# Attention's planned time scaled by 0.9 and 1.1 for ten tiles, and the ends of the later tiles in eight half groups

## The chip, the cores and the metric

The kernel runs on one core of a Trainium2 chip. A core has five engines that work side by side, each through its own queue in order: TensorE (PE, matrix multiplication; its loads of weights are shown as PEld), VectorE (DVE), ScalarE (ACT), GpSimd (POOL) and SyncE (SP, which issues DMAs). Sixteen DMA engines move data. The metric is the device time of one execution in microseconds (us); the kernel before has a median of 1754.32 us over three runs, from 1749.43 to 1756.26.

## The reference

One layer of a graph network with 4096 nodes of 512 features, all in 32 bit floats. The adjacency matrix is sparse: about one entry in 256 is set, and the diagonal always is. Eight heads of 64 features attend from the target rows to the neighbours alone, then come a residual, a second normalisation, a feed-forward part with 2048 hidden units, another residual with x and a last normalisation.

```python
hs = layer_norm(h_source, ln1_scale, ln1_bias)
ht = layer_norm(h_target, ln1_scale, ln1_bias)
q = (ht @ Wq + bq).reshape(T, H, HD) / jnp.sqrt(jnp.float32(HD))
k = (hs @ Wk + bk).reshape(S, H, HD)
v = (hs @ Wv + bv).reshape(S, H, HD)
logits = jnp.einsum('thd,shd->hts', q, k)
logits = jnp.where(edge_mask[None] != 0, logits, NEG)
probs = jax.nn.softmax(logits, axis=-1)
ctx = jnp.einsum('hts,shd->thd', probs, v).reshape(T, D)
ht = ht + ctx @ Wo + bo
ht = layer_norm(ht, ln2_scale, ln2_bias)
ff = jax.nn.gelu(ht @ W1) @ W2
return ht + ff
...
x = _layernorm(x + layer(x, h_target, adj, ...), axis=-1)
```

## The kernel before

The kernel never forms the dense 4096 x 4096 logits. It makes a list of neighbours for each row, sorts the rows by the number of their neighbours, and treats them in 32 tiles of 128 rows. A tile has as many slots as its longest row has neighbours (its cap, from 11 to 39; 603 slots in all). For each slot, one indirect DMA, which POOL issues, gathers the key and the value row of that neighbour for all 128 rows of the tile.

The first stage, until about 290 us, projects x to keys and values, which go to a table in DRAM, while ACT and DVE read the adjacency of the first 16 x 128 rows (part A), and part of that of the rest (part B), and make their lists. The second stage, which the change touches, weaves four streams together: attention over the 32 tiles, the feed-forward part over 18 groups of tiles, the rest of part B's lists with their sort, and the loads of half of the feed-forward weights.

Tiles are numbered from 0 in the code. Tiles 0, 1, 2 and 31 are groups of their own; tiles 3 to 30 go in pairs, (3, 4), (5, 6), and so on. Their caps, from tile 0: 11, 13, 14, 15, 15, 16, 17, 17, 18, 19, 19, 20, 22, 23, 24, 39, 12, 38, 13, 24, 14, 23, 15, 22, 15, 20, 16, 19, 17, 18, 17, 18. Tiles 0 to 15 belong to part A, the others to part B. Part B's records are put in order by 16 scatters that POOL issues (L880), spaced by 4.5 units of planned time, and loaded again by SP (L1008).

**The order of the work.** A function `_weave` writes down the program's order. Each stream is a Python generator that emits some instructions and then yields the planned time that these are to stand for. The stream whose planned clock is lowest goes next. A stream that yields None sleeps until another has gone on, and its clock is then at least that one's. The planned times are only weights: a pair of tiles has 60 units (`UNIT`) of feed-forward and 60 units of attention, where `PACE` doesn't say otherwise. So `PACE` sets how much feed-forward stands between two steps of attention in PE's queue, and in the others.

**Attention** (`attention`) goes through a tile in groups of three slots, and yields twice in each group: each yield ends a half group. DVE multiplies the gathered keys with the queries (L1287) and adds them up (L1293), ACT takes the exponential (L1300), DVE scales two of the three values with it (L1234) and ACT the third (L1268), DVE adds values in pairs in some groups (L1238, L1241), and PE turns the scaled values and adds them up in PSUM (`cps`, L1247). Gathers are requested four groups ahead into a ring of 17 slots, 20 in part B. The planned time of a half group is `cost` times its slots; `cost` comes from L1276, and L1277 and L1278 scale it: 0.7 for tiles 1 to 4, 0.85 for tiles 5 to 8, 1 from tile 9 on.

**A tile's end** (`finish`) is a generator that goes one step at each half group of the tiles that follow. DVE sums and inverts the weights' sums (L1123 to L1130), ACT spreads them out (L1133), PE turns them (L1139), ACT copies the result (L1141), DVE multiplies `cps` with it (L1144), PE turns the target rows into PSUM and adds the output projection (L1153, L1157), ACT copies the sum (L1163), DVE takes the moments (L702, L685), POOL the power -1/2 (L692), DVE the shift (L697), ACT normalises (L1179), PE turns (L1188) and ACT writes `h2T` (L1192). Between the steps it waits for a number of half groups that depends on `slow`: 1 + slow before L1139, 1 + slow before L1144, 1 + 3 slow before L1153, one each before L1163, the moments, L692 and L697, and 1 + slow before L1188. In all that is 8 half groups with `slow` = 0 and 14 with `slow` = 1. `slow` (L1120) is 0 for tiles 0 to 6 and 1 for the others.

**Feed-forward** (`feed`) of a group can only begin when its `h2T` has been written; until then the stream sleeps, and a group from the fourth on that has slept adds 3 units. It has 16 steps for a pair: 8 of hidden units (PE L1407, then the gelu on ACT, L1410), and 8 of outputs (PE L1416), with PE's transposes for the residual (L1441) among them. Its end (`end`) normalises, and POOL scatters the rows to the output.

Of the kernel before, what the change touches and what calls it, by code (L numbers as in the profile page):

```python
# [443 lines left out]
def adj_resnorm_kernel(  # L444
# [88 lines left out]
    with tc.tile_pool(name="keep", bufs=1) as keep:  # L533
# [17 lines left out]
        with ExitStack() as late:  # L551
# [171 lines left out]
            def behind(ins):  # L723
                return tc.issue_after(ins[-1]) if ins else nullcontext()
# [349 lines left out]
            def step(gens, i):  # L1074

                if i in gens and next(gens[i], StopIteration) is StopIteration:
                    del gens[i]

            def request(k):


                while issued[0] <= min(k + AHEAD, len(SG) - 1):
                    issue(issued[0])
                    mine = set(range(place[issued[0]], place[issued[0]] + SG[issued[0]][2]))
                    for m in range(max(k - len(held_up), 0), issued[0]):
                        assert not mine & set(range(place[m], place[m] + SG[m][2]))
                    issued[0] += 1
# [28 lines left out]
            def finish(i, p, cps, group, hs, mv):  # L1116


                rec, tq, cap = recs[i], tqs.pop(i), TILES[i][1]
                slow = 0 if i < QUICK else 1  # L1120
                first = i == 0

                nc.vector.scalar_tensor_tensor(p[:, :cap, :], rec[:, E0:E0 + cap].unsqueeze(2)  # L1123
# [72 lines left out]
            def go_on():  # L1196
                for i in list(fronts):
                    step(fronts, i)
# [18 lines left out]
            def attention():  # L1217


                tails, pend, turns = [], [], []  # L1220

                def advance():
                    go_on()
                    for t in list(tails):
                        if next(t, StopIteration) is StopIteration:
                            tails.remove(t)

                def values(i, j0, n, kv, p, cps, after):

                    m = n - 1 if n == S else n
                    v4 = kv[:, :m, D:].rearrange("p j (h d) -> p j h d", h=H)
                    nc.vector.tensor_tensor(v4, v4, p[:, j0:j0 + m, :].unsqueeze(3)  # L1234
                                            .to_broadcast([P, m, H, HD]), ALU.mult)
                    slots = list(range(n))
                    if m > 1 and i >= ADDS and TILES[i][1] < (HEAVY if i > NA else 23):
                        nc.vector.tensor_add(kv[:, 0, D:], kv[:, 0, D:], kv[:, 1, D:])  # L1238
                        slots.remove(1)
                        if n == S and i >= DENSE and j0 // S % 2:  # L1240
                            nc.vector.tensor_add(kv[:, 0, D:], kv[:, 0, D:], kv[:, S - 1, D:])  # L1241
                            slots.remove(S - 1)

                    def turn():
                        for j in slots:
                            for c in range(KC):
                                nc.tensor.matmul(cps[:, c, :], kv[:, j, D + c * P:D + (c + 1) * P],  # L1247
                                                 ident, is_transpose=True,
                                                 start=j0 + j == 0 and c == 0,
                                                 stop=j0 + n == TILES[i][1] and j == slots[-1],  # L1250
                                                 skip_group_check=True)
                        if after is not None:
                            tails.append(after)

                    turns.append(turn)
                    held_up[:] = turns

                def add_up():
                    while turns:
                        turns.pop(0)()  # L1260
                    held_up.clear()

                def by_scalar(kv, lg):
                    pa = sp.tile([P, H], F32, name="pa")
                    nc.scalar.activation(pa, lg[:, S - 1, :], AF.Exp)
                    for hd in range(H):
                        v = kv[:, S - 1, D + hd * HD:D + (hd + 1) * HD]
                        newest[:] = [nc.scalar.mul(v, v, pa[:, hd:hd + 1]).ins]  # L1268

                request(0)  # L1270
                yield 0.0
                k = 0
                for group in GROUPS:
                    hs = []
                    mv = sp.tile([P, 2, 2], F32, name="mv2")
                    cost = 0.5 * UNIT * len(group) / 2 / sum(TILES[i][1] for i in group)  # L1276
                    if 0 < group[0] < 9:  # L1277
                        cost *= PACE[group[0] > 4]  # L1278
                    for i in group:
                        cps = ps.tile([P, KC, P], F32, name="cps", bufs=2)  # L1280
                        while k < len(SG) and SG[k][0] == i:
                            _, j0, n = SG[k]
                            while i not in tqs:
                                step(fronts, i)
                            kv, tq = kvs.pop(k), tqs[i]
                            with behind(closing[:1 if j0 < 2 * S else 2]):
                                nc.vector.tensor_tensor(kv[:, :n, :D], kv[:, :n, :D],  # L1287
                                                        tq[:, :D].unsqueeze(1)
                                                        .to_broadcast([P, n, D]), ALU.mult)
                            lg = sp.tile([P, S, H], F32, name="lg")  # L1290
                            latest[:] = [lg[:, 0, 0:1]]
                            with behind(closing if j0 == S else []):
                                logits[:] = [nc.vector.tensor_reduce(  # L1293
                                    lg[:, :n, :],
                                    kv[:, :n, :D].rearrange("p j (h d) -> p j h d", h=H),
                                    AX.X, ALU.add).ins]
                            if i != 1:
                                closing.clear()
                            if j0 > 0:
                                nc.scalar.activation(p[:, j0:j0 + n, :], lg[:, :n, :], AF.Exp)  # L1300
                            add_up()
                            if k > 0:
                                request(k - 1)
                            advance()
                            yield cost * n
                            if pend:
                                values(*pend.pop())
                                if i < QUICK:
                                    add_up()
                                if i < QUICK or i > NA:  # L1310
                                    request(k)
                            advance()
                            if j0 == 0:
                                p = sp.tile([P, MAXE, H], F32, name="p", bufs=1)
                                nc.scalar.activation(p[:, :n, :], lg[:, :n, :], AF.Exp)
                            if n == S:
                                by_scalar(kv, lg)
                            last = j0 + n == TILES[i][1]
                            after = finish(i, p, cps, group, hs, mv) if last else None
                            pend.append((i, j0, n, kv, p, cps, after))  # L1320
                            yield cost * n
                            k += 1
                values(*pend.pop())
                add_up()
                while tails:
                    advance()
                    yield 3.0
                verdict()
# [138 lines left out]
            DENSE = 21  # L1467
            QUICK = 7
            UNIT = 60.0
            PACE = (0.7, 0.85)  # L1470

            ed = all_edges()
            steps = 2 * NQ + 1
# [41 lines left out]
            def fill():  # L1515
# [4 lines left out]
                for cost in _take(ed, FILL * steps):  # L1520
                    yield cost

            att = attention()
            _weave((projections(), 0), (prepare(), 0), (fill(), 0))
            src.close()
# [58 lines left out]
```

## Time and profile before

| what | value |
|---|---|
| median of the runs | 1754.32 us |
| the profiled execution's own time | 1755.7 us |
| its span, from first to last instruction | 1754.0 us |
| last matmul's end | 1742.5 us |
| granted clock of PE, mean | 0.981 |
| PE idle in the whole span | 98 us |
| L1407 and L1416 on PE, hidden and output matmuls | 468.9 and 461.2 us |
| L1247 on PE, turning the values | 243.7 us |
| gathers of keys and values on POOL (L994) | 603, 800.6 us |
| last step of attention (L1247) | 1629 us |

The span is the time on the core between its first and last instruction; the profiled execution's own time has 1.7 us around it. Busy times of different engines run side by side and don't add up. PE's records are pipelined, so the start of one matmul to the start of the next tells its price better than its own length.

### The profile page before, as it was taken

The page shows a single profiled execution, that of the slowest core. Times are in us where ns is not written, and L with a number is a line of the kernel's source. Part 1 is how long each engine was busy: PE and PEld are TensorE (multiplying, and loading weights), DVE is VectorE, ACT ScalarE, POOL GpSimd, SP SyncE. Part 2 cuts the span into 40 slices and gives each one's busy share as a digit, 9 for nine tenths or more (in the row PEclk, how much of TensorE's full clock was granted, in tenths as well). Part 3 has the DMA queues.
Part 4 walks back from the last instruction along what each step waited for, and adds up shares of the span by engine and source line. Part 5 has one row for each costly group of instructions (what it writes and reads, how often), then busy time and mean ns, then how long its engine had stood idle before and what let it go on. Part 6 is the DMA issues. An engine that isn't in the chain of part 4 may idle for free. (4 is left out here: it accounts for less than half of the span.)

```text
span 1754.0 us, 22757 instructions
## 1 busy us (share of the span) xinstructions
PE 1655.5 (94%) x6994; PEld 1078.4 (61%) x6994; DVE 1421.2 (81%) x2450; ACT 1232.7 (70%) x3134; POOL 1034.1 (59%) x824
## 2 busy tenths in 40 slices
PE   7999896999899999998899999999999999999997
PEld 3444443776676766666566667666666666666665
DVE  6887796879898999996788989988989788999300
ACT  5776673679678888685667878777878677878311
POOL 1000155667666677888687787777787866784101
PEclk9999998899999999999999999999999999999999
DMA  9999988978888897778788888887877767775000
GB/s 353 360 391 358 363 275 307 336 265 291 281 293 307 298 341 251 245 231 260 235 305 288 294 267 289 298 272 228 270 247 255 253 223 258 223 259 191 24 1 27
DMA packets 141611, 461.02 MB, mean 263 GB/s; under 512 B 18036, under 2 KB 23048, under 8 KB 141480
## 3 DMA queue, kind: packets, MB, share of 16 engines
q0 software_dynamic: 96272, 342.33, 58.2%
q1 hardware_dynamic: 39504, 98.26, 15.8%
q10 hardware_dynamic: 5704, 18.89, 2.7%
q8 instruction: 58, 0.95, 0.2%
q14 instruction: 73, 0.60, 0.1%
HBM read 430.61 MB, written 28.79 MB: 262 GB/s over the span
## 5 line engine op out<-in xcount | busy, mean ns | idle before, releaser
L994 POOL DMA_INDIRECT kv<-kvd,rec x603 | 800.6, 1328 | 288.7 <-issue 117.6
L1407 PE MATMUL pf<-h2T,w 128*128 128x256 f32 (+1 forms) x2304 | 468.9, 358 | 6.1 <-ACT h2T L1192 5.9
L1416 PE MATMUL po<-w,gt 128*128 128x512 f32 x1024 | 461.2, 593 | 5.6 <-ACT gt L1410 5.6
L1407 PEld LDWEIGHTS pf<-h2T,w 128*128 128x128 f32 x2304 | 394.9, 192 | 67.9 <-issue 17.7
L1287 DVE TENSOR_TENSOR kv<-kv,tq 128x1536 f32<-128x1536 f32 (+2 forms) x211 | 351.9, 1678 | 70.5 <-DMA kv<-kvd,rec 65.7
L1268 ACT ACTIVATE kv<-kv,pa 128x64 f32<-128x64 f32 x1520 | 390.9, 336 | 4.1
L1293 DVE TENSOR_REDUCE lg<-kv 128x24 f32<-128x1536 f32 (+2 forms) x211 | 350.9, 1669 | 0.3
L1416 PEld LDWEIGHTS po<-w,gt 128*128 128x128 f32 x1024 | 187.2, 190 | 201.4 <-issue 192.2
L1247 PEld LDWEIGHTS cps<-ident,kv 128*128 128x128 f32 x1844 | 218.4, 143 | 93.7 <-issue 44.4
L1234 DVE TENSOR_TENSOR kv<-kv,p 128x1024 f32<-128x1024 f32 (+1 forms) x211 | 251.6, 1196 | 19.3 <-ACT p L1300 19.2
L1247 PE MATMUL cps<-ident,kv 128*128 128x128 f32 x1844 | 243.7, 278 | 24.2 <-DVE kv L1234 17.6
L692 POOL TENSOR_TENSOR n_rs<-n_ve,mhalf 128x2 f32<-128x2 f32 (+2 forms) x53 | 57.6, 1086 | 338.4 <-DVE n_ve L685 157.7
L740 ACT ACTIVATE kv<-kv 128x1024 uint8<-128x1024 int32 x128 | 134.4, 1053 | 56.4 <-DMA kv<-in_adj_dram 22.9
L1410 ACT ACT_TABLE_LOAD x108 | 138.6, 1283 | 1.9
L1410 ACT ACTIVATE gt<-pf 128x512 f32<-128x512 f32 x128 | 76.4, 597 | 75.4 <-PE pf L1407 71.9
L1157 PE MATMUL t<-wo,rb 128*128 128x512 f32 x256 | 119.6, 611 | 5.3 <-DVE rb L1144 5.3
L956 PE MATMUL pq<-wk,h2T 128*128 128x512 f32 x256 | 121.2, 618 | 3.0 <-ACT tq L958 1.6
L956 PE MATMUL pq<-wv,h2T 128*128 128x512 f32 x256 | 115.5, 594 | 3.7 <-ACT kv L958 2.2
L1047 PE MATMUL t<-wq,tq 128*128 128x512 f32 x256 | 115.0, 593 | 2.9 <-ACT tq L1040 2.9
L749 DVE MAX8 cand<-kv 128x8 uint16<-128x171 uint16 (+1 forms) x384 | 108.4, 326 | 1.0
L1300 ACT ACTIVATE p<-lg 128x24 f32<-128x24 f32 (+2 forms) x179 | 38.9, 217 | 92.4 <-DVE lg L1293 89.5
L956 PEld LDWEIGHTS pq<-wv,h2T 128*128 128x128 f32 x256 | 48.3, 190 | 66.3 <-issue 56.9
(165 smaller groups left out, 1587.6 us busy)
## 6 DMA issues: line engine op xcount, KB each, us to landing
kv<-in_adj_dram SPq DMA_DIRECT2D x128, 512.0 KB, 6.8
kvd<-tq ACTq DMA_DIRECT2D x23, 512.0 KB, 7.2
kv<-kvd,rec POOLq DMA_INDIRECT x603, 5.9
kv<-in_L_gnn_h_target_dram SPq DMA_DIRECT2D x32, 256.0 KB, 6.8
w<-in_L_gnn_W_dram SPq DMA_DIRECT2D x8, 1024.0 KB, 9.7
kv<-in_x_dram SPq DMA_DIRECT2D x15, 512.0 KB, 8.2
kvd<-kv ACTq DMA_DIRECT2D x9, 512.0 KB, 7.7
rest_d<-gid SPq DMA_DIRECT2D x32, 96.0 KB, 5.1
```

The source lines that it names most:

```text
L740: nc.scalar.activation(sg, a, AF.Sign, accum_out=dpart[:, i, h:h + 1])
L956: nc.tensor.matmul(pkv, hT[:, kc, j * P:(j + 1) * P], w[:, kc, :], start=kc == 0, stop=kc == KC - 1)
L994: issues[:] = [nc.gpsimd.indirect_dma_start(out=dst, out_offset=None, in_=table[:, :], in_offset=bass.IndirectOffsetOnAxis(ap=idx, axis=0) ...
L1157: nc.tensor.matmul(pa, ct[:, c, :], wo[:, c, :], start=False, stop=c == KC - 1, skip_group_check=True)
L1234: nc.vector.tensor_tensor(v4, v4, p[:, j0:j0 + m, :].unsqueeze(3) .to_broadcast([P, m, H, HD]), ALU.mult)
L1247: nc.tensor.matmul(cps[:, c, :], kv[:, j, D + c * P:D + (c + 1) * P], ident, is_transpose=True, start=j0 + j == 0 and c == 0, stop=j0 + n ...
L1268: newest[:] = [nc.scalar.mul(v, v, pa[:, hd:hd + 1]).ins]
L1287: nc.vector.tensor_tensor(kv[:, :n, :D], kv[:, :n, :D], tq[:, :D].unsqueeze(1) .to_broadcast([P, n, D]), ALU.mult)
L1293: logits[:] = [nc.vector.tensor_reduce(lg[:, :n, :], kv[:, :n, :D].rearrange("p j (h d) -> p j h d", h=H), AX.X, ALU.add).ins]
L1407: nc.tensor.matmul(pf[:, k, :], w1[(f0 + k) // KC][:, kc, (f0 + k) % KC * P:((f0 + k) % KC + 1) * P], h2T[:, kc, :w], start=kc == 0, stop= ...
L1410: nc.scalar.activation(gt, pf, AF.Gelu_apprx_tanh)
L1416: nc.tensor.matmul(po[j], gt[:, k, j * P:(j + 1) * P], w2[(f0 + k) // KC][:, (f0 + k) % KC, :], start=False, stop=f0 + k == FC - 1, skip_g ...
```

## The change

Three edits of constants and conditions; no instruction is added or taken away.

```diff
-                slow = 0 if i < QUICK else 1
+                slow = 0 if i < QUICK or i > 10 else 1
...
-                    if 0 < group[0] < 9:
-                        cost *= PACE[group[0] > 4]
+                    if 0 < group[0] < 19:
+                        cost *= PACE[(group[0] > 4) + (group[0] > 8) + (group[0] > 10)]
...
-            PACE = (0.7, 0.85)
+            PACE = (0.7, 0.85, 0.9, 1.1)
```

`group[0]` is the first tile of a group. The pair (9, 10) gets a planned time of 54 units for its attention instead of 60, and the four pairs (11, 12) to (17, 18) get 66 each. Tiles up to 8 and from 19 on keep theirs. The ends of tiles 11 to 31 take 8 half groups instead of 14; those of tiles 7 to 10 keep 14, and those up to tile 6 keep 8.

## The prediction

> **What bounds the kernel now.** I read the first part of the page, then the busy time of all engines in stretches of 50 us, then the waits of PE between 600 and 1640 us, and last the timeline around the longest of them.
>
> ```profile
> span 1754.0 us, 22757 instructions
> PE 1655.5 (94%) x6994; PEld 1078.4 (61%) x6994; DVE 1421.2 (81%) x2450; ACT 1232.7 (70%) x3134; POOL 1034.1 (59%) x824
> ```
>
> PE is the bound: its work and its idle time add up to the span. The change takes no work away, so the only things it can move are PE's idle 98 us and the clock that PE gets. The stretches (columns: PE, PEld, DVE, ACT, POOL busy, PE's clock, DMA share, GB/s) show where idle time is left:
>
> ```profile
> 650.00:700.00 50.00, 47.25 (x215) 32.13 (x215) 49.90 (x92) 39.10 (x100) 35.08 (x23) 1.00 0.81 271
> 700.00:750.00 50.00, 48.60 (x204) 31.44 (x203) 48.40 (x60) 35.59 (x95) 41.79 (x29) 1.00 0.74 241
> 750.00:800.00 50.00, 45.75 (x205) 31.69 (x204) 38.38 (x48) 34.94 (x93) 40.35 (x34) 1.00 0.76 242
> 800.00:850.00 50.00, 45.30 (x210) 31.94 (x211) 41.73 (x39) 34.08 (x96) 37.48 (x31) 0.97 0.74 233
> 850.00:900.00 50.00, 40.69 (x187) 28.60 (x186) 36.16 (x38) 33.13 (x103) 36.47 (x31) 0.93 0.82 273
> ...
> 1600.00:1650.00 50.00, 50.00 (x212) 33.94 (x211) 34.76 (x76) 30.31 (x80) 4.96 (x5) 1.00 0.11 35
> 1650.00:1700.00 50.00, 50.00 (x186) 33.30 (x185) 3.23 (x12) 10.99 (x22) 5.26 (x6) 1.00 0.07 21
> ```
>
> In 650 to 750 DVE is full (lists and tiles 9 and 10, counted from 0). From 750 to 900 PE idles 18.3 us of 150 and DVE is not full. From 1650 on there is feed-forward alone and PE never waits. Some 55 us of PE's idle time fall before 600 us or behind the last matmul, where the change does nothing.
>
> ```profile
> PE t L1037 <- ACT tq L1033: 10.4, 3, 7.9
> PE cps L1247 <- DVE kv L1238: 6.2, 6, 2.2
> PE cps L1247 <- DVE kv L1234: 6.1, 2, 5.9
> PE pf L1407 <- ACT h2T L1192: 5.9, 5, 2.2
> PE t L1188 <- ACT h L1179: 5.4, 4, 3.0
> ```
>
> (total us, times, longest.) Nothing waits at L1157, the output projection at the tile's end. The timeline of PE gives the two long gaps, and the price of a feed-forward step:
>
> ```profile
> 774.92 3.62 PE L1407 MATMUL pf<-h2T,w 128*128 128x256 f32 x16
> 778.38 3.60 PE L1416 MATMUL po<-w,gt 128*128 128x512 f32 x8
> 781.81 1.04 PE L1247 MATMUL cps<-ident,kv 128*128 128x128 f32 x8
> ...
> 804.70 2.82 PE L1247 MATMUL cps<-ident,kv 128*128 128x128 f32 x12 [5.88 <-DVE kv L1234]
> ...
> 879.60 1.11 PE L1037 MATMUL t<-ident,tq 128*128 128x128 f32 x4 [7.88 <-ACT tq L1033]
> ```
>
> Behind both stands POOL: DVE waits 7.9 and 8.9 us for gathers just before, since POOL issues one gather per 1.25 us without a break and has 16 record scatters (L880, 730 to 853 us) among them.
>
> **The planned clocks.** A pair's feed-forward is 8 hidden steps of 778.38 - 774.92 = 3.46 us, 8 output steps of 3.43 and 1.04 of transposes: 56.2 us for 60 planned units, 0.94 us each. A pair of tiles has 60 units of attention too. Before, the pairs from tile 9 on end at 276, 336, 396, 456, 516; after, at 270, 336, 402, 468, 534 and 18 later from there. Feed-forward of group g becomes ready a tile end behind. Fourteen half groups of some 2.4 units are 34, eight are 19: for groups from tile 19 on the 18 later and the 15 sooner nearly cancel. Followed through the weave's rule, feed-forward of group g (from 4 on) starts at 60 g - 45.1 in both until it sleeps once, at group 15 before (starting at 862.7), at group 10 after (560.7); its last group starts at 982.7 before and 980.7 after. So feed-forward is neither starved nor moved; attention is moved against it, first 6 units forward, then 24 back. The stretch of feed-forward alone at the end loses 18 x 0.94 = 17 us, which the middle gets.
>
> **Term A, 0.9 on tiles 9 and 10.** PE gets 5.6 us less feed-forward there, while DVE is the bound. DVE idles 4.4 us in 600 to 750 (50 - 47.30 in the first row not shown, then 0.10 and 1.60). If attention moves up into that, PE loses 5.6 - 4.4 = 1.2 us; if DVE takes no more, 5.6. I take 1.2, as DVE's idle time is there in the row. The lists' work is put behind attention by as much and has slack until the scatters.
>
> **Term B, 1.1 on tiles 11 to 18.** Four pairs get 5.6 us more feed-forward each, 22.5 in all, from 752 to about 1080 us. PE's gaps there, from the timeline: 0.86, 2.20, 5.88, 1.22, 7.88 up to 880, then 1.63, 2.20, 3.02, 2.31, in all 27.2. While POOL and DVE set the pace, each us of matmuls put in takes a us of gap. Up to 880 the first pair and two thirds of the second add 9.5 against 18.0; behind it 12 against 9.2, of which I leave 1 for handovers. Gain 9.5 + 8.2 = 17.7. Bounds: nothing, where the gaps are fixed distances between two instructions that both move, and 22.5. In the planned span of the scatters (301 to 369) attention reaches tile 14 three units later, so they share POOL with some 45 slots' gathers instead of 50: 5 x 1.25 = 6 us that help the same gaps and aren't added.
>
> The clock: in 805 to 810 us its row has 0.75 and in 875 to 885 0.58 and 0.74; some 3.3 us of matmuls ran at half speed behind each long gap, 1.6 us lost each. With 8.5 us of gaps left I count one: -1.6 (0 to -3.2). The Trainium skill (TensorE: Matmul & The Clock Gate, Part 1: The HAM clock gate) says that the clock halves after an idle window of about 3.4 us. The trace bears it out roughly (3.02 us at 1047 is not followed by it, 3.10 at 323 is), and by the rule both losses would vanish only if both gaps fall below that.
>
> **Term C, eight half groups.** Nothing is added; ACT's copies L1133 and L1141, DVE's product L1144, PE's L1139, L1153 and L1157, then the norm (DVE, POOL's power L692 past some gathers, ACT L1179) and PE's L1188 come sooner. No DMA is among them. The transposes L1139 and the projection L1157 stand 2 half groups apart instead of 6. Six early tile ends already run so; one waited:
>
> ```profile
> 454.09 0.60 PE L1139 MATMUL t<-ident,rb 128*128 128x128 f32 x4
> ...
> 463.80 0.58 ACT L1141 COPY rb<-t 128x512 f32<-128x512 f32 x1
> ...
> 464.41 0.69 DVE L1144 TENSOR_TENSOR rb<-cps,rb 128x512 f32<-128x512 f32 x1
> ...
> 465.15 5.89 PE L1157 MATMUL t<-wo,rb 128*128 128x512 f32 x8 [5.28 <-DVE rb L1144]
> ```
>
> ACT had 9.7 us of other work ahead. While PE waits there, the next attention transposes and feed-forward are queued behind it, and with them POOL's free slots. For the 21 tile ends from 11 on I took from the timeline how long L1139 to the end of L1144 lasts now (1.4 to 8.7 us) and a third of the distance from L1139 to L1157 (4.1 to 8.8). The first is longer at tiles 12, 14, 15, 16, 21 and 23, by 1.7, 3.7, 1.5, 1.1, 0.9 and 1.8: 10.7 us. At L1188 one half group of 2.8 us goes; where ACT's L1179 ended less than that ahead (groups 7, 8, 9 and 15, by 1.3, 0, 0 and 1.9) 8.0 us are lost. Of the 18.7, 15.1 are in the stretch where B takes away the lateness; I scale these with its idle time, 9.5 of 27.2, to 5.3, and keep 3.6: +8.9. Bounds: 0, as five of the six early ends show, and by the sixth: 5.28 and 3.4 us of half clock work, over six ends 1.45 a tile, 30 us in 21.
>
> At no cost: some 2.4 more gelus stand among exponentials, two table loads of 1283 ns each, 6 us of ACT, hidden by its 11 to 16 idle us in every 50. The Trainium skill (ScalarE: Activation LUTs, Table sets: the hidden batching unit) speaks against it: calls of one set belong together, and a switch is put at 2.66 us with a drain, which would make it 13. The timeline shows gelu 20 ns behind a load's end, so no drain.
>
> **The sum.** 1.2 - 17.7 - 1.6 + 8.9 = -9.2 against the profiled execution's 1755.7: 1746.5. That one was 1.4 above the median shown, so against the median 1745.1; I say 1745.
>
> **Rivals.** *The tile ends take the place of the gaps (slower).* For it: ACT and DVE run in order, and the end at 465 us; against it: lists burdened ACT then (its stretch 460 to 465 has 4.94 of 5 busy), and later ACT is busy 34 of 50. At 1.45 us for each of the 21 ends, and half of B: 1.2 - 8.9 + 30 = +22, 1776 against the median; at two thirds of that price +12, 1766. It decides from (17.7 + 1.6 - 1.2) / 21 = 0.86 us a tile on. *The gaps stay (no change).* The gaps follow POOL's queue and the record loads, which move along with attention; at 863 us POOL itself waited 5.1 us for a record load behind the last scatter. Against it: POOL's load per matmul falls. Then 1.2 + 3.6 less a few us: 1750 to 1759. *Nothing of C comes and B is whole:* 1.2 - 22.5 - 3.2 = -24.5, 1730.
>
> **How the numbers follow.** Forecast with its own range of 1736 to 1747: 0.38; the whole gain 0.10; no change 0.27; slower 0.25. About 0.5% is what a measurement of this kernel can tell from nothing, 1745.5 to 1763.1; the forecast's upper edge lies within it by little. So faster 0.47, same 0.28, slower 0.25. The range 1729 to 1769 leaves out the worst of the slower case and little of the gain.
>
> **What would show it.** B right: no PE gap over 3.5 us at 780 to 900, no row under 0.95 in the clock there, idle time of PE from 750 to 1080 under 12 us. A right: 1 to 6 us more PE idle in 650 to 750. C right: waits at L1157 and L1188 together of 5 to 14 us; over 20 and the slower rival has it. The stretch with DVE nearly idle at the end should be some 95 us long instead of 112. The forecast is wrong if that stretch shrinks and PE's idle time doesn't: then gaps moved instead of closing.

## The result and the profile after

The changed kernel takes 1746.65 us (median of 22 runs, 1739.93 to 1756.12) against 1753.93 us of the kernel before in the same jobs: ratio 0.9962, 95% interval 0.9949 to 0.9974. By the ratio that is 6.7 us less (the medians differ by 7.3), where 9.2 were predicted.

The first part of the page, of the changed kernel:

```profile
span 1739.8 us, 22750 instructions
PE 1654.6 (95%) x6994; PEld 1075.0 (62%) x6994; DVE 1421.7 (82%) x2450; ACT 1236.4 (71%) x3136; POOL 994.5 (57%) x824
```

The work is the same, 1654.6 us of PE against 1655.5; what went is idle time. The profiled execution is one of the shortest, 5 us under the median: it was 3 us ahead at 560 us, while the order on PE first differs near 617 us, so some 11 of the 14 us between the two spans arise where the kernels differ. The medians say 7; the rest is the spread between executions. The stretches of 50 us (columns as before):

```profile
650.00:700.00 50.00, 46.90 (x206) 31.47 (x205) 49.90 (x88) 42.73 (x112) 30.25 (x27) 1.00 0.82 285
700.00:750.00 50.00, 47.73 (x202) 30.90 (x200) 50.00 (x67) 38.69 (x98) 36.34 (x26) 1.00 0.68 224
750.00:800.00 50.00, 49.11 (x223) 34.39 (x223) 39.77 (x48) 37.95 (x103) 40.10 (x34) 1.00 0.77 247
800.00:850.00 50.00, 42.48 (x182) 27.90 (x181) 39.62 (x37) 33.95 (x94) 33.88 (x30) 0.93 0.71 231
850.00:900.00 50.00, 50.00 (x241) 36.13 (x240) 35.62 (x38) 33.52 (x88) 40.16 (x32) 1.00 0.86 290
...
1600.00:1650.00 50.00, 48.65 (x210) 32.93 (x209) 40.68 (x85) 35.39 (x89) 11.60 (x11) 1.00 0.24 81
1650.00:1700.00 50.00, 50.00 (x172) 31.43 (x171) 2.03 (x7) 6.38 (x12) 0.58 (x1) 1.00 0.02 6
```

From 750 to 900 PE now idles 8.4 us instead of 18.3, and nothing at all in the last 50 of these. In 650 to 750 it idles 5.4 instead of 4.2. The stretch 800 to 850 got worse, with a clock of 0.93. Attention's last matmul (L1247) ends at 1642.5 us of 1728.6, so feed-forward stands alone for 86 us. Before it was 104: the table ahead of the prediction gives 1629 us for attention's last step, but the trace has its last L1247 at 1638.1.

Where the feed-forward went can be counted in the two traces, with the prediction's prices of a step (3.46, 3.43 and 1.04 us). Between the last L1247 of tile 10 and that of tile 18 PE does 245.3 us of it instead of 224.6. Of these 20.7 us, 3.5 come from tiles 9 and 10 and 17.2 from the end. PE's idle time between the same two points fell from 29.6 to 14.2 us.

The waits of PE between 600 and 1640 us (total, times, longest):

```profile
PE t L1157 <- DVE rb L1144: 8.9, 2, 6.0
PE pf L1407 <- ACT h2T L1192: 7.7, 6, 2.4
PE cps L1247 <- DVE kv L1238: 7.1, 9, 1.7
PE t L1188 <- ACT tq L1040: 2.0, 2, 1.5
PE po L1416 <- ACT gt L1410: 1.4, 1, 1.4
```

The long waits for gathered values and for the queries are gone, and L1157, where nothing waited, leads the list. The other engines say that the relief is real. These are a wait of DVE, before and after, and one of POOL, before and after, in the same stretch:

```profile
DVE kv L1287 <- DMA kv<-kvd,rec: 48.7, 17, 8.9
...
DVE kv L1287 <- DMA kv<-kvd,rec: 29.3, 14, 5.3
...
POOL kv L994 <- PE cps L1247: 44.5, 51, 3.4
...
POOL kv L994 <- PE cps L1247: 69.3, 58, 6.2
```

DVE waits 29.3 us for gathers instead of 48.7, and POOL waits 69.3 us for PE to free slots instead of 44.5: POOL is ahead of PE more of the time. The longest gap that is left, at tile 12's end, in the timeline:

```profile
794.94 0.60 PE L1139 MATMUL t<-ident,rb 128*128 128x128 f32 x4
...
799.89 0.58 ACT L1141 COPY rb<-t 128x512 f32<-128x512 f32 x1
...
805.96 0.69 DVE L1144 TENSOR_TENSOR rb<-cps,rb 128x512 f32<-128x512 f32 x1
...
806.70 4.63 PE L1157 MATMUL t<-wo,rb 128*128 128x512 f32 x5 [5.98 <-DVE rb L1144]
```

It is a gap of the kind that stood at 465 us before, where ACT alone was late and DVE followed at once. Here ACT comes to its copy 4.3 us after the transposes and DVE to its product 5.5 us after the copy, and PE, which has the projection two half groups on in its queue, waits for it.

### The profile page after: what moved, and what is told of

Its sections match the earlier page's. It is cut to its first block, busy times and chain, and to the rows that moved or that the text cites. A ratio compares the mean times of both kernels' runs of the same rounds, so it can differ in the third digit from the quotient of the medians.

```text
span 1739.8 us, 22750 instructions
## 1 busy us (share of the span) xinstructions
PE 1654.6 (95%) x6994; PEld 1075.0 (62%) x6994; DVE 1421.7 (82%) x2450; ACT 1236.4 (71%) x3136; POOL 994.5 (57%) x824
## 5 line engine op out<-in xcount | busy, mean ns | idle before, releaser
L994 POOL DMA_INDIRECT kv<-kvd,rec x603 | 775.9, 1287 | 320.9 <-issue 115.3
L1407 PE MATMUL pf<-h2T,w 128*128 128x256 f32 (+1 forms) x2304 | 471.3, 359 | 7.8 <-ACT h2T L1192 7.7
L1407 PEld LDWEIGHTS pf<-h2T,w 128*128 128x128 f32 x2304 | 394.1, 192 | 64.9 <-ACT h2T L1192 12.5
L1247 PEld LDWEIGHTS cps<-ident,kv 128*128 128x128 f32 x1844 | 216.2, 142 | 89.7 <-issue 51.3
L1247 PE MATMUL cps<-ident,kv 128*128 128x128 f32 x1844 | 242.1, 276 | 17.5 <-DVE kv L1234 10.4
L692 POOL TENSOR_TENSOR n_rs<-n_ve,mhalf 128x2 f32<-128x2 f32 (+2 forms) x53 | 48.5, 915 | 313.4 <-DVE n_ve L685 170.7
L1157 PE MATMUL t<-wo,rb 128*128 128x512 f32 x256 | 123.8, 629 | 12.5 <-DVE rb L1144 12.5
```

The lines of the kernel that those rows point to most:

```text
L994: issues[:] = [nc.gpsimd.indirect_dma_start(out=dst, out_offset=None, in_=table[:, :], in_offset=bass.IndirectOffsetOnAxis(ap=idx, axis=0) ...
L1157: nc.tensor.matmul(pa, ct[:, c, :], wo[:, c, :], start=False, stop=c == KC - 1, skip_group_check=True)
L1407: nc.tensor.matmul(pf[:, k, :], w1[(f0 + k) // KC][:, kc, (f0 + k) % KC * P:((f0 + k) % KC + 1) * P], h2T[:, kc, :w], start=kc == 0, stop= ...
```

## The experiments

Each edit is shown against the changed kernel. All ratios are to the kernel before, with their 95% intervals.

| run | tiles 9, 10 | tiles 11 to 18 | half groups of the ends | ratio |
|---|---|---|---|---|
| before | 1 | 1 | 14 | 1 |
| changed | 0.9 | 1.1 | 8 from tile 11 | 0.9962 (0.9949 to 0.9974) |
| e1 | 0.9 | 1.1 | 14 | 0.9982 (0.9968 to 0.9997) |
| e2 | 1 | 1 | 8 | 1.003 (1.0013 to 1.0048) |
| e3 | 0.9 | 1 | 8 | 1.0111 (1.0096 to 1.0126) |
| e4, e11 | 0.9 | 1.1 | 14 to tile 14, then 8 | 0.9942 (0.9924 to 0.996), 0.9941 (0.9924 to 0.9958) |
| e5 | 0.95 | 1.1 | 8 | 0.9983 (0.9966 to 1.0001) |
| e6 | 0.9 | 1 | 14 | 1.0073 (1.0048 to 1.0099) |
| e7 | 0.9 | 1.05 | 8 | 1.0029 (1.0012 to 1.0045) |
| e8 | 0.9 | 1.1, and 0.95 on 19, 20 | as e4 | 0.9974 (0.9959 to 0.9988) |
| e9 | 0.9 | 1 | 14, lists from 64 | 1.0077 (1.0065 to 1.0089) |
| e10 | 0.9 | 1.1 | 10 | 1.0021 (1.0006 to 1.0036) |
| e12 | 0.9 | 1.1 | as e4, lists from 67 | 1.0018 (1.0004 to 1.0033) |

The trace of each run gives PE's idle time between 560 us and its last matmul, from the starts and ends of its matmuls, and half of the busy time that fell into records of half clock:

| profiled run | idle us | lost to half clock | sum | last matmul ends |
|---|---|---|---|---|
| before | 43.9 | 2.9 | 46.8 | 1742.5 |
| changed | 30.4 | 5.9 | 36.3 | 1728.6 |
| e1 | 33.6 | 10.0 | 43.7 | 1737.3 |
| e2 | 41.3 | 8.3 | 49.6 | 1743.3 |
| e3 | 47.7 | 7.6 | 55.3 | 1749.7 |
| e4 | 34.5 | 4.9 | 39.4 | 1733.8 |
| e5 | 33.6 | 9.7 | 43.3 | 1736.9 |
| e6 | 47.7 | 13.1 | 60.8 | 1755.0 |
| e7 | 40.9 | 12.7 | 53.6 | 1744.0 |
| e8 | 30.4 | 8.1 | 38.5 | 1735.2 |
| e9 | 39.7 | 17.2 | 56.9 | 1749.9 |
| e10 | 38.1 | 7.3 | 45.4 | 1738.9 |
| e11 | 30.3 | 6.0 | 36.3 | 1728.5 |
| e12 | 39.0 | 9.4 | 48.4 | 1743.2 |

The last column less the sum is 1690 to 1697 us in every row. So what these executions differ by behind 560 us is PE's gaps and its half clock, to within that spread of 6 us, which is as large as the change's gain. That says where the time went, not why. And each row is a single execution: those of the changed kernel, e3 and e10 are 5, 9 and 5 us faster than their medians, so the ratios above decide what an edit is worth.

**e1, the planned times alone.**

```diff
-                slow = 0 if i < QUICK or i > 10 else 1
+                slow = 0 if i < QUICK else 1
```

> The change with the tiles' ends as before (fourteen half groups from tile 7 on): terms A and B without C. Theory 1, the prediction's sum of independent terms: 1.2 - 17.7 - 1.6 = -18 us, ratio to before 0.990. Theory 2, B needs C: without the sooner ends feed-forward of the groups behind tiles 15 to 18 isn't ready in time (followed through the weave it sleeps at groups 9, 10 and 15 and its last group starts at planned 1000.7 instead of 982.7), so nothing is moved from the end into the middle: ratio 0.998 to 1.010, and the stretch of feed-forward alone at the end stays near 110 us. Theory 3, the gain is C's: ratio 1.00.

Theory 1's 0.990 is far outside the interval; the time is at the lower edge of theory 2's. And feed-forward stands alone for 104.1 us, as in the kernel before. A stretch of it:

```profile
1600.00:1650.00 50.00, 50.00 (x206) 33.75 (x205) 30.96 (x76) 27.45 (x74) 4.07 (x4) 1.00 0.07 24
```

In 1600 to 1650 DVE works 31 us here and 41 in the changed kernel: attention is over sooner against feed-forward. Nothing was moved from the end into the middle, as theory 2 had followed through the weave, where the groups sleep until their late h2T. Tiles 11 to 18 still have 13.8 us of feed-forward more than before, but 3.5 of it come from tiles 9 and 10 and 10.4 from tiles 19 to 31. What is left of the gain is local.

**e2, the ends alone.**

```diff
-            PACE = (0.7, 0.85, 0.9, 1.1)
+            PACE = (0.7, 0.85, 1.0, 1.0)
```

> Only the ends of tiles 11 to 31 in eight half groups, attention's planned times as before: term C alone. Theory 1: a loss, 8.9 us where B relieves the middle and up to 18.7 where it doesn't, ratio 1.005 to 1.011, with waits at L1157 and L1188 of 10 to 20 us together. Theory 2: the same sign, as nothing is moved. Theory 3, the sooner ends themselves free PSUM and the buffer of L1133 and so bring the gain: ratio 0.994 to 0.997.

A loss, 5.3 us, so theory 3 falls; it is smaller than theory 1 had it. Its waits, over the same part of PE's time:

```profile
PE t L1157 <- DVE rb L1144: 8.4, 3, 6.0
PE cps L1247 <- DVE kv L1234: 6.9, 3, 5.8
```

The gap at 801 us is still there (5.78), and one of 6.01 at L1157 (916 us) has come. Against this, feed-forward alone shrank to 96 us, as the sleep before group 15 went. By the table PE even idles less than before, 41.3 us against 43.9; what its sum has more is half clock, 8.3 us against 2.9. The mean granted clock says the same over all executions: 0.980 in the twelve of e2, 0.982 in the 23 of the kernel before beside them, which is up to 4 us.

**e3, without 1.1.**

```diff
-            PACE = (0.7, 0.85, 0.9, 1.1)
+            PACE = (0.7, 0.85, 0.9, 1.0)
```

> The change without 1.1: tiles 9 and 10 at 0.9, tiles 11 to 18 at 1.0, ends in eight half groups (terms A and C). Theory 1 and 2: ratio 1.005 to 1.012, 1 to 6 us above the run with the ends alone. The stretch of feed-forward alone at the end would be the longest of all, near 118 us. Theory 3: ratio 0.994 to 0.997, the whole gain without 1.1.

The ratio (of four runs) is as theories 1 and 2 said, but by another share: it is 14 us over e2, where term A was to be 1 to 6. The end was not the longest (99.8 us). From e3 to the changed kernel, 1.1 is worth 26 us.

**e4 and e11, the first four long ends back.**

```diff
-                slow = 0 if i < QUICK or i > 10 else 1
+                slow = 0 if i < QUICK or i > 14 else 1
```

> The change with the ends of tiles 11 to 14 in fourteen half groups again, those of 15 to 31 in eight. In the changed kernel the two long waits of PE (5.98 at 807 us, 2.93 at 912 us) stand at L1157 of tiles 12 and 14. If they are the price of the short distance (term C), they go with the half clock behind them: 8.9 us of waits and up to 5 us of clock, ratio to before 0.988 to 0.992. If they are lateness that shows wherever PE meets DVE next, the time stays that of the changed kernel, 0.995 to 0.998.

> The version with the ends from tile 15 on once more, for a narrower interval than 0.9924 to 0.9960: the same, 0.993 to 0.996. Under 0.9949 it would be outside the interval of the changed kernel (0.9949 to 0.9974).

Twice 0.994, faster than the kernel before by 10 us, and between what the two theories gave for e4. The interval of e11 and that of the changed kernel overlap (0.9949 to 0.9958), so that it beats the change too is likely and not shown. The waits of e11:

```profile
PE pf L1407 <- ACT h2T L1192: 9.0, 6, 2.6
...
PE po L1416 <- ACT gt L1410: 6.1, 3, 3.4
PE cps L1247 <- DVE kv L1234: 3.6, 3, 3.1
```

L1157 is off the list, but 3.1 us come back at the attention matmul (797 us) and 3.4 at a gelu (937 us). Some of the lateness was the short ends' price, some only showed there.

**e5 and e6, more and less of 0.9.**

```diff
-            PACE = (0.7, 0.85, 0.9, 1.1)
+            PACE = (0.7, 0.85, 0.95, 1.1)
```

> The change with 0.95 instead of 0.9 on tiles 9 and 10. Theory 1 (0.9 costs 1 to 6 us of feed-forward cover where DVE is full, so half of it comes back): ratio to before 0.993 to 0.996. Theory 2 (0.9 is worth its price when 1.1 follows: it brings attention forward, so that tiles 11 to 14 start sooner against the scatters and the record loads): ratio 0.997 to 1.000.

Theory 1 falls by little, and theory 2's number holds: with 1.1 behind it, 0.9 is 3.7 us better than 0.95, though the intervals overlap. Theory 2's reason is not shown by that. e6 has 0.9 alone, with the ends as before:

```diff
-                slow = 0 if i < QUICK or i > 10 else 1
+                slow = 0 if i < QUICK else 1
...
-            PACE = (0.7, 0.85, 0.9, 1.1)
+            PACE = (0.7, 0.85, 0.9, 1.0)
```

> Only 0.9 on tiles 9 and 10; tiles 11 to 18 at 1.0 and the ends as before: term A alone. The run without 1.1 was 14 us above the one with the ends alone, where the prediction gave A 1 to 6 us. If A itself has that price, ratio 1.006 to 1.010; if the price comes from the ends being short while attention is ahead of feed-forward, ratio 1.000 to 1.003.

Term A by itself costs 12.8 us. Three stretches and two waits of e6 show where:

```profile
650.00:700.00 50.00, 46.91 (x210) 32.21 (x209) 49.90 (x85) 41.22 (x107) 30.70 (x28) 1.00 0.81 284
700.00:750.00 50.00, 47.54 (x200) 30.17 (x199) 50.00 (x71) 38.08 (x97) 37.58 (x28) 1.00 0.71 238
750.00:800.00 50.00, 43.39 (x190) 28.81 (x188) 38.54 (x44) 33.10 (x96) 40.64 (x33) 0.96 0.70 235
```

```profile
PE cps L1247 <- DVE kv L1234: 14.4, 2, 8.6
...
PE t L1188 <- ACT h L1179: 7.6, 4, 4.3
```

In 650 to 750 PE loses 1.4 us more than before, as predicted. The rest comes later, and most of it in this execution is the clock. The gap at 802 us has grown from 5.9 to 8.6 and one of 5.8 stands at 900, but that of 7.9 at 880 is gone: from 750 to 1100 us PE idles 26.4 us, no more than before (28.2). The records have 37 us of half clock behind 560 us instead of 10. So of the 14.0 us that PE's sum is longer than before, 10.2 are half clock and 3.8 idle time. This execution had a lower clock than most; the mean over the seven of e6 is 0.978, over the 30 of the kernel before beside them 0.981, which is some 5 us of the 12.8 at most.

**e7, half of 1.1.**

```diff
-            PACE = (0.7, 0.85, 0.9, 1.1)
+            PACE = (0.7, 0.85, 0.9, 1.05)
```

> The change with 1.05 instead of 1.1 on tiles 11 to 18: half of B. If each us of feed-forward put into the middle takes a us of gap (the prediction's rule), the time lies halfway between the run without 1.1 (1.011) and the changed kernel (0.996): 1.002 to 1.005. If the gain hangs on the long gaps that halve the clock, it comes at once or not at all: 0.995 to 0.998, or over 1.007.

About halfway between e3 and the changed kernel (their mean is 1.0037): half of the pace brings about half of the gain, which does not hang on one gap. That each us of matmuls takes a us of gap is not shown by it. From e3 to e7, and again from e7 to the changed kernel, tiles 11 to 18 get 10.4 us more feed-forward; in the traces PE's idle time there falls by 4.3 us at the first step and by 11.4 at the second.

**e8, a lead for attention.** Against e4:

```diff
+                    elif group[0] == 19:
+                        cost *= 0.95
```

> A version to beat both: ends of tiles 15 to 31 in eight half groups, tiles 9 and 10 at 0.9, 11 to 18 at 1.1, and the pair of tiles 19 and 20 at 0.95, which lets attention lead feed-forward by 3 more units from there. In the run with the ends from tile 15, PE waited 10.6 us in 8 times at L1407 for h2T, since feed-forward takes each h2T as soon as it is written. If the lead takes these away: ratio 0.988 to 0.992. If the lateness shows at another wait: 0.993 to 0.996.

It brought nothing, and 5 to 6 us of e4's gain went, so both theories' ranges were missed. The waits for h2T fell from 9.3 us in e4 to 2.1, but those for a gelu rose from 5.5 to 8.3. A wait at L1407 of 2 us each is no gap that can simply be taken out.

**e9, are the lists the cause of e6?** Against e6:

```diff
-            WAIT = 70.0
+            WAIT = 64.0
```

> As the run with 0.9 alone (1.0073), but part B's lists, their sort and scatters start at planned 64 instead of 70, so that from tile 11 on attention and lists stand as in the kernel before to each other, both 6 units ahead of feed-forward. Theory L (0.9 costs 13 us since attention outruns the lists, and their DVE work and scatters fall on tiles 11 and 12): ratio 0.998 to 1.002, tile 12's end near 790 us instead of 802, the 8.6 us gap at 802 under 5. Theory F (it costs as 6 units of feed-forward are missing in PE's queue from there on): ratio 1.005 to 1.010, the gaps stay.

The gap came down to 6.3 us, as theory L had it in part, but it ended at 806 us instead of 802, and tile 12's last L1247 at 796.3 instead of 790.1. The time is that of e6; theory F's number holds. It doesn't prove F: PE's order differs from that of e6 from about 411 us on, and tiles 9 and 10 have 3.4 us less feed-forward, so more than the lists moved. Nor does PE idle more than in the kernel before (39.7 us against 43.9); what the table has more is half clock, 17.2 us.

**e10, two half groups more before the projection.**

```diff
-                for _ in range(0 if first else 1 + 3 * slow):
+                for _ in range(0 if first else 3 if i > 10 else 1 + 3 * slow):
```

> The change with the ends of tiles 11 to 31 in ten half groups: two more between the product L1144 and the projection L1153, the rest as in the change. If the waits at L1157 (8.9 us in 2 and the half clock behind) are the price of the short ends, they go and the ratio is 0.990 to 0.994. If what counts is when h2T is ready (feed-forward sleeps when it is late, 2 half groups are some 5 units), the waits go and the time doesn't: 0.997 to 1.002, with a stretch of feed-forward alone at the end of over 90 us.

The waits at L1157 fell from 8.9 to 0.9 us and the time got 10 us worse, just above what the second theory gave; feed-forward alone lasted 92 us.

```profile
PE t L1188 <- ACT h L1179: 8.3, 4, 7.2
```

PE now waits 7.2 us at once for the normalised rows (at 835 us), further on in the same end.

**e12, the lists sooner.** Against e4, `WAIT` at 67.

> The version with the ends from tile 15 on and the lists 3 planned units sooner. By theory L the lists' load on tiles 11 and 12 goes down a little and with it the remaining gap of 2.5 us at 799: ratio 0.990 to 0.994. If DVE, full from 600 to 750 us, only gets the lists' work sooner: 0.995 to 0.999.

Neither: 1.0018, 13 us over e4. Its trace has a gap of 9.1 us at 873 and one of 4.8 at 742, both of attention's matmul behind DVE. Three units in the lists' place cost as much here as 0.9 did in e6, while the six of e9 changed nothing against e6. Why, no run shows.

## Why the prediction was right, and where its steps were wrong

The forecast held in direction and size (-9.2 predicted, -6.7 measured), and the mechanism that it named first is shown: feed-forward put into tiles 11 to 18 (20.7 us, 22.5 predicted) closes PE's gaps there, and most of it comes out of the end, whose stretch is 18 us shorter (17 predicted). The terms, however, didn't hold singly.

- **Term B (-17.7 and -1.6 of clock).** Measured -16 us with long ends (e6 to e1) and -26 us with short ones (e3 to the change). Both stand beside 0.9, so they include what 1.1 takes back of A's price. The rule of a us of gap for each us of matmuls was too high in the traces: in the change 20.7 us more feed-forward took 15.4 us of idle time in tiles 11 to 18. From 750 to 1080 us idle time fell from 28.2 to 11.6, where I had asked for under 12.
- **Term A (1.2, at most 5.6) is the step that failed.** It measured 12.8 us alone and 14 with the short ends. I priced it in its own stretch, where it was right (1.2 to 1.4 us), and took it that the price ends there. But by the planned clocks attention then stays 6 units ahead of feed-forward through the tightest stretch, until something gives them back, and part of the price there is the clock: in e6's trace 10.2 us more of half clock, with no more idle time from 750 to 1100 us. In the change 1.1 gives the 6 units back, and then 0.9 costs nothing that shows (e5). Whether it is the missing matmuls or the work of the lists that falls on tiles 11 and 12 stays open; e9's number is that of the first, and it moved too much to settle it. 1.1 with the short ends and without 0.9 wasn't tried.
- **Term C (+8.9) had the right waits, but beside A and B it was no cost.** L1157 and L1188 waited 11.5 us together, in the range I gave, and 6.1 more than before; alone the ends cost 5.3 us. But beside A and B they bring 3.5 us (e1 to the change, with intervals that overlap), or 7 where they begin at tile 15 (e1 to e4, intervals apart). My planned clocks had the reason, that 18 units later and 15 sooner nearly cancel; in the sum I left out that without the second, none of B's matmuls comes out of the end (e1).
- **No gap over 3.5 us at 780 to 900, no clock under 0.95:** wrong, by the 5.98 us at 807 and 0.93. I had counted one half clock loss as left; the profiled execution has three records behind 560 us, 5.9 us against 2.9 before. Over all executions the clock did get better, as the term said: its mean is 0.983 in the 22 of the changed kernel and 0.981 to 0.982 in the 70 of the kernel before beside the experiments.
- **The rivals.** The slower one named the right place, L1157, but the waits there and at L1188 grew by 6 us together over 21 ends, 0.3 a tile, under the 0.86 from which it decides. That the gaps simply stay is wrong for the one at 880, which is gone, and for the idle time as a whole; at 805 one as long as before has come in its place, now at L1157.

Along e6, e1 and the changed kernel the terms measured +12.8, -16.0 and -3.5 us, where +1.2, -19.3 and +8.9 were predicted. So the sum came out since A's error and C's, some 12 us each, have opposite signs. That was luck: a good total, made of three terms of which one held.

## What to carry to other kernels

Where streams are woven by planned times, an edit of one stretch shifts everything behind it until another edit takes the shift back: follow the lead of one stream over the other to the end, and price each edit with the others in place. Filling a busy engine's gaps with other work needs that work to be ready there; a shorter chain that makes it ready can lose by itself and still be what part of the gain hangs on. And before counting single waits, add up the bound engine's idle time and its slow clock: if the rest is nearly constant over all variants, as here, that sum says where the time went, and whether a loss is idle time at all. Here most of e2's loss, and a good part of e6's, was clock.

## What the runs showed of the hardware

The clock's records behind 560 us are stretches of 3.4, 6.8 or (once each in e1, e6 and e12) 10.2 us at half clock, and nearly all stand at one of PE's longer gaps. The length of the gap doesn't settle it: in the changed kernel 2.93 us at 912 was followed by one, and so were 0.49 and 2.36 us close together at 1300; in the kernel before 3.02 us at 1048 was not, and in e3 3.79 us at 957 was not. The kernel of e4 and e11 shows both at the same place. The first line is of e4, the second of e11:

```profile
940.07 3.70 PE L1416 MATMUL po<-w,gt 128*128 128x512 f32 x8 [3.41 <-ACT gt L1410]
...
937.06 6.63 PE L1416 MATMUL po<-w,gt 128*128 128x512 f32 x8 [3.41 <-ACT gt L1410]
```

After the same wait the same eight matmuls took 3.70 us once and, at half clock, 6.63 the other time. So what a gap costs in clock differs from one execution to the next, and the runs show no fixed price: from 2.9 us beside 43.9 of idling (before) to 17.2 beside 39.7 (e9).
